# An edge-gated graph layer on one core: a new order of gates and products, of the first loads and of the table rows, and shorter edge lists

## The chip, the cores and the metric

The kernel runs on one core of one Trainium2 chip. The metric is the device time in microseconds, lower is better. An engine's instructions run in the order in which the program lists them; between engines semaphores hold an instruction until what it reads is there. The engines are TensorE (PE, with its weight loads as PEld), VectorE (DVE), ScalarE (ACT), GpSimd (POOL) and SyncE (SP), and 16 DMA engines move the data.

## The reference

One layer of a graph network over a fixed adjacency matrix. x holds 16 batches of 1024 nodes with 256 features, adj is 1024 × 1024 with about nine entries in a row, and the sum over neighbours is gated per edge and per batch:

```python
pre_u = einsum('bud,dk->buk', h, W1[:d]);  pre_v = einsum('bvd,dk->bvk', h, W1[d:])
hidden = relu(pre_u[:, :, None, :] + pre_v[:, None, :, :] + b1)
S = sigmoid(einsum('buvk,ko->buvo', hidden, W2)[..., 0] + b2[0])
a_t = einsum('buv,bud->bvd', S * A, h)
m_t = einsum('uv,bud->bvd', A, h) * h
z = beta1 * h + beta2 * (a_t @ Wa + ba) + beta3 * (m_t @ Wm + bm)
```

The kernel computes S only where A has an entry.

## The kernel before

**Tiles.** Work is cut into 32 blocks. A block is one group of four batches and one tile of 128 target nodes; each block has 10 steps, numbered n = 0 to 319 over the whole kernel (`T` = 10, `total` = 320). Groups 0 and 1 come first (six tiles each, then the last two of each), then groups 2 and 3. A step treats 128 edge slots, one edge per partition, for four batches.

**A step.** `fetch(n)` (L518, GpSimd) gathers 128 rows of 8 KB, one per edge slot, from a table in device memory that holds pre_u and h side by side. Eight buffers (`NF`) hold fetched rows, so that eight fetches are ahead. `fetch_val` (L385, GpSimd) gathers the adjacency values. `expand(n + 2)` (L607, PE) spreads pre_v of the target nodes over the edge slots into one of two PSUM buffers pc. `add(n + 1)` (L639, DVE) sums the two, `gate(n)` (four of L647, DVE) does relu and the dot product with W2, one batch each; ACT then does the sigmoid gt (L650), four scalings left (L652), and `left_adj(n + 1)` (L617), which prepares the next step's adjacency. `aggregate` (L664, PE) multiplies left with the fetched h into the accumulators, which L672 copies to ev at the end of each half.

**Products.** `products(n)` issues PE's other work of a step: pieces of table rows (`rows`: w_u products at L445, copied by ACT at L461 to one of two single tab buffers, written to the table by SP at L465), the halves of pre_v of the next block (`halves`: L445, L449, ACT copies L482, L483, L489), and the end of the block before. `turn_over` transposes ev (L682), ACT copies it to LT (L685), and one or two steps later DVE multiplies part of it by h (L696). `block_end` does the products with w_a and w_m (L713), ACT copies the result (L718), a step later DVE adds it to h_blk (L719), and SP writes it out. All these PE results go through two PSUM buffers "misc".

**Lists.** For each of the eight tiles `lists(vt)` finds the edges and their slots: L252 to L375, mostly small DVE operations, with a few matmuls and one ACT copy. Lists 0 to 3 (`EARLY`) run ahead of the first step, by the `script`; lists 4 to 7 run in pieces between gates (`fill`), begun at the steps in `start_list`. A list's first act is to load its key (L244), for lists 4 to 7 from GpSimd.

**Order.** Each engine's order is the program's, written by hand. `after(step, f)` makes f due at a step; `do(n)` issues what is due on the queue that f names (L719 and L696 on DVE; the table writes and the outputs on SP). For the main loop (L857 to L925) the order of a step is: gather in, expand(n + 2), fill, a `do(n)` ahead of the others at step 8, products(n), add(n + 1), gate(n) with the ACT work, left_adj(n + 1), do(n). In the last block only (n ≥ total − T), expand and products come after the gate. `plan` says at which step a block's hT is loaded and at which two steps its table rows are made; for the rows of group 1, L775. Ahead of the loop the script issues the eight first fetches in a row ("f"), and SP then has two hT loads and, at n = 1, w_a and w_m (L888, L889).

Of the kernel before, what the change touches and what calls it, by code (L numbers as in the profile page):

```python
# [13 lines left out]
P = 128  # L14
# [3 lines left out]
def kernel(  # L18
# [58 lines left out]
    RC = 5 + S  # L77
# [42 lines left out]
    late = fixed([P, 1], "late")  # L120
    nc.vector.tensor_scalar(late, row, float(W), None, ALU.is_ge)
    soon = fixed([P, 1], "soon")
    nc.vector.tensor_scalar(soon, row, float(W), None, ALU.is_lt)
# [77 lines left out]
    rest = const.tile([P, NT], FP, name="rest")  # L201
    nc.gpsimd.memset(val, 0.0)
# [38 lines left out]

    def lists(vt):
# [3 lines left out]
        R = lst.tile([P, RC], FP, name="R", bufs=4)  # L246
        top = R[:, 5:5 + S]
        count = lst.tile([P, 1], FP, name="count", bufs=4)
# [6 lines left out]
        nc.scalar.activation(unread, key, AF.Sign, accum_out=count)  # L255
# [24 lines left out]
        yield "op"  # L280
        nc.vector.tensor_scalar(R[:, 2:3], row, float(N), float(vt * P * N), ALU.mult, ALU.add)
        yield "op"
        nc.vector.memset(R[:, 3:4], 1.0)
        yield "op"
        nc.vector.tensor_copy(R[:, 4:5], inw)
# [17 lines left out]
        held = lst.tile([P, 1], FP, name="held", bufs=4)  # L303
# [7 lines left out]
        yield "op"  # L311
        nc.vector.tensor_tensor(rest[:, vt:vt + 1], count, held, ALU.subtract)
# [4 lines left out]
        none = lst.tile([P, 1], FP, name="none", bufs=4)  # L317
        nc.vector.tensor_scalar(none, held, 0.0, float(N + 1), ALU.is_equal, ALU.mult)
        yield "op"
        nc.vector.tensor_scalar(held, held, -1.0, None, ALU.add)  # L320
        yield "op"
        nc.vector.scalar_tensor_tensor(mark, slot, first, mark, ALU.is_ge, ALU.mult)
        yield "op"
        last = lst.tile([P, 1], FP, name="last", bufs=4)
        nc.vector.scalar_tensor_tensor(used, nth, held, top, ALU.is_equal, ALU.mult, accum_out=last)
        yield "op"
        nc.vector.tensor_tensor(thr[:, vt:vt + 1], last, none, ALU.add)
# [4 lines left out]
        for w, mine in enumerate((soon, late)):  # L332
            nc.vector.tensor_scalar(RR[:, w, :], R, mine, None, ALU.mult)
# [21 lines left out]
        nc.vector.tensor_tensor(eq, eq, L[:, :, 5:], ALU.mult)  # L355
# [7 lines left out]
        nc.vector.tensor_tensor(k_of, L[:, :, 2], k_of, ALU.subtract)  # L363
        yield "op"
        nc.vector.scalar_tensor_tensor(k_of, L[:, :, 3], -BIG, k_of, ALU.mult, ALU.add)
        yield "op"
        nc.vector.tensor_scalar(vidx[:, sl].rearrange("p w j -> p (w j)"), k_of, BIG + N, None, ALU.add)
# [4 lines left out]
        for i in range(2):  # L372
            nc.vector.tensor_tensor(
                onehot[:, sl].rearrange("p w (q i) v -> p w q i v", i=2)[:, :, :, i, :],
                place.unsqueeze(1).to_broadcast([P, NW, Q, V]),  # L375
                col[:, :, i:i + Q, 4:5].to_broadcast([P, NW, Q, V]), ALU.is_equal)
            if i == 0:
                yield "op"
# [49 lines left out]
    def load_hT(k):  # L428
        g, nt = k
        if k in aside_:  # L430
            hTs[k] = hta.tile([P, GB, DC, P], FP, name="hT_")
        else:
            hTs[k] = hT_of[k] = hT_free.pop(0)
        nc.sync.dma_start(hTs[k].rearrange("p b c n -> p (b c) n"),
                          xT_rows[:, g * GB * DC:(g + 1) * GB * DC, nt * P:(nt + 1) * P])
# [105 lines left out]
    for i in range(COPIES):  # L541
# [3 lines left out]
              "h 2 1 1", "h 2 2 3 u", "2 f 2 2 w h h h", "m 3 w 3 3 3")  # L545
# [14 lines left out]
    for t, turns_ in enumerate(script):  # L560
        step = t - 100
        do(step)
        for c in turns_.split():
# [8 lines left out]
            elif c == "h":  # L572
                go(parts, step)
            elif c == "v":
                fetch_val(T)
                spread(b1_p, b1_b)
                next(parts)
            elif c == "f":
                for n in range(NF):
                    fetch(n)  # L580
            elif c == "u":
                fetch_val(3)
            elif c == "m":
                load_mark(0)
            elif c == "w":
                warm(6)
            else:
                next(made[int(c)], None)
# [177 lines left out]
    start_list = dict(zip((0, 16, 48, 88), range(EARLY, NT)))  # L766
# [8 lines left out]
    plan(turn[NT:], ((0, 1, 8), (1, 9, 12), (9, 18, 19), (13, 22, 28), (20, 29, 32), (29, 38, 39), (33, 42, 48), (40, 49, 51)))  # L775
# [8 lines left out]
    def made_rows(n):  # L784
        nonlocal piece, last
        if n in loads:
            if loads[n] in begun and loads[n][0] == 1:
                aside_.remove(loads[n])
            load_hT(loads[n])
            if loads[n] not in begun:  # L790
                copy_h(loads[n])
                begun.add(loads[n])
# [7 lines left out]
    def products(n, k, s):  # L800
# [10 lines left out]
        if ROOM <= n < total - T:  # L811
            if s in (8, 9):
# [28 lines left out]
    ROOM, MORE, LISTS = 10, 3, 110  # L841
    ahead = NF
# [17 lines left out]
    for n in range(total + 2):  # L860
# [10 lines left out]
        if n < total - T:  # L871
            expand(n + 2)
            if n >= ROOM:
                fill(n, False)
                if s == 8:
                    do(n)
# [8 lines left out]
        if n >= total - T and n + 2 < total:  # L885
            expand(n + 2)
        if n == 1:
            w_a = load_weights(Wa, "w_a", nc.sync)  # L888
            w_m = load_weights(Wm, "w_m", nc.sync)  # L889
# [23 lines left out]
        if n < ROOM:  # L913
            fill(n, False)
        if n >= total - T:
# [6 lines left out]
        if n == 120:  # L922
            nc.gpsimd.partition_all_reduce(longest, rest, P, bass_isa.ReduceOp.max)
# [116 lines left out]
```

## Time and profile before

| | us |
|---|---|
| timed, median of 3 | 1110.08 |
| timed, lowest and highest | 1110.04, 1113.46 |
| profiled execution, its own time | 1097.05 |
| span of that execution | 1095.2 |

The mean granted TensorE clock in that execution was 0.979. The profile is of one execution. In its rows the first number is the start in us, the second the duration in us, and what stands in brackets is how long the engine sat idle before the instruction and what released it. A wait row names the waiting instruction, then what it waited for, with the total in us, the count and the longest. Start and length of the blocks, from the first add of each in the timeline:

| block | start | length | DVE idle in it |
|---|---|---|---|
| 0 | 63.48 | 39.07 | 10.74 |
| 1 | 102.56 | 35.65 | 0.14 |
| 2 | 138.20 | 37.99 | 2.17 |
| 3 | 176.19 | 35.85 | 2.49 |
| 4 | 212.04 | 30.68 | 0.97 |
| 5 | 242.72 | 37.60 | 4.44 |
| 6 | 280.32 | 33.55 | 0.00 |
| 7 | 313.87 | 30.55 | 1.09 |
| 8 | 344.42 | 30.26 | 1.30 |
| 9 | 374.68 | 32.81 | 0.00 |
| 10 | 407.49 | 37.31 | 3.05 |
| 11 | 444.80 | 30.58 | 1.27 |
| 12 to 22, mean of each | | 30.15 | 1.23 |
| 23 to 30, mean of each | | 29.92 | 0.99 |
| 31, to the end | 1046.47 | 48.78 | 9.44 |

### The profile page before, as it was taken

The page shows a single profiled execution, that of the slowest core. Times are in us where ns is not written, and L with a number is a line of the kernel's source. Part 1 is how long each engine was busy: PE and PEld are TensorE (multiplying, and loading weights), DVE is VectorE, ACT ScalarE, POOL GpSimd, SP SyncE. Part 2 cuts the span into 40 slices and gives each one's busy share as a digit, 9 for nine tenths or more (in the row PEclk, how much of TensorE's full clock was granted, in tenths as well). Part 3 has the DMA queues.
Part 4 walks back from the last instruction along what each step waited for, and adds up shares of the span by engine and source line. Part 5 has one row for each costly group of instructions (what it writes and reads, how often), then busy time and mean ns, then how long its engine had stood idle before and what let it go on. Part 6 is the DMA issues. An engine that isn't in the chain of part 4 may idle for free.

```text
span 1095.2 us, 24089 instructions
## 1 busy us (share of the span) xinstructions
PE 1029.3 (94%) x7645; PEld 735.7 (67%) x7645; DVE 1020.8 (93%) x3487; ACT 862.0 (79%) x2616; POOL 465.5 (42%) x453
## 2 busy tenths in 40 slices
PE   7876998998999999999999999999999999999986
PEld 7744766776667767677777777777766666666653
DVE  8878999998999999999999999999999999999994
ACT  3435777786889877888988888888888888888873
POOL 2746676472456324554334333333343332333320
PEclk9887999999999989999999999999999999999999
DMA  9998999999999999999999999999999999999991
GB/s 289 330 399 282 331 361 355 398 377 378 388 356 396 399 391 348 380 392 402 406 401 405 395 409 391 392 395 401 358 384 341 353 340 334 337 347 353 347 328 43
DMA packets 149032, 394.56 MB, mean 360 GB/s; under 512 B 18224, under 2 KB 96048, under 8 KB 112688
## 3 DMA queue, kind: packets, MB, share of 16 engines
q0 software_dynamic: 50240, 300.11, 69.8%
q1 hardware_dynamic: 85360, 79.71, 22.7%
q10 hardware_dynamic: 13296, 13.11, 3.7%
q8 instruction: 63, 1.03, 0.4%
q14 instruction: 73, 0.60, 0.1%
HBM read 396.93 MB, written 50.33 MB: 408 GB/s over the span
## 4 chain that ended last, share of the span: by engine, by line
PE 58%; DVE 17%; ACT 12%; DMA 8%; issue 4%; POOL 0%; DVEq 0%; SPq 0%; ACTq 0%; POOLq 0%
PE misc L713 16%; PE acc L664 14%; PE misc L445 13%; PE pc L607 9%; DVE fetched L647 7%; DVE fetched L639 6%; ACT left L652 3%; PE misc L682 2%; DMA fetched<-table,uidx 2%; PE misc L449 2%; DMA hT<-in_xT_dram 2%; ACT X L489 1%; ACT LT L718 1%; DMA table<-tab 1%; DMA key<-in_adjT_dram 1%
## 5 line engine op out<-in xcount | busy, mean ns | idle before, releaser
L518 POOL DMA_INDIRECT fetched<-table,uidx x320 | 344.9, 1078 | 534.8 <-PE acc L664 361.8
L647 DVE SCALAR_TENSOR_TENSOR fetched<-fetched,w_b 128x256 f32<-128x256 f32 x1280 | 477.1, 419 | 0.0
L639 DVE TENSOR_TENSOR fetched<-fetched,pc 128x1024 f32<-128x1024 f32 x320 | 387.9, 1212 | 11.5 <-PE pc L607 5.0
L652 ACT ACTIVATE left<-left,gt 128x32 f32<-128x32 f32 (+1 forms) x1280 | 299.5, 305 | 10.4
L664 PE MATMUL acc<-fetched,left 128*32 128x256 f32 x4096 | 287.3, 389 | 19.4 <-ACT left L652 19.3
L607 PE MATMUL pc<-X,mark 128*128 128x512 f32 x640 | 244.8, 464 | 16.2 <-DVE fetched L639 14.6
L664 PEld LDWEIGHTS acc<-fetched,left 128*32 128x32 f32 x4096 | 133.9, 110 | 131.9 <-ACT left L652 42.3
L607 PEld LDWEIGHTS pc<-X,mark 128*128 128x128 f32 x640 | 106.0, 191 | 96.4 <-issue 35.4
L650 ACT ACTIVATE gt<-sc,b_b 128x4 f32<-128x4 f32 x320 | 95.9, 300 | 57.9 <-DVE fetched L647 55.1
L713 PE MATMUL misc<-w_m,LT 128*128 128x256 f32 x496 | 117.3, 379 | 0.0
L713 PE MATMUL misc<-w_a,LT 128*128 128x256 f32 x496 | 117.2, 379 | 0.0
L445 PE MATMUL misc<-w_v,hT 128*128 128x256 f32 x448 | 107.6, 384 | 0.0
L713 PEld LDWEIGHTS misc<-w_a,LT 128*128 128x128 f32 x496 | 94.0, 190 | 15.1 <-ACT LT L685 0.4
L713 PEld LDWEIGHTS misc<-w_m,LT 128*128 128x128 f32 x496 | 94.1, 190 | 14.8
L385 POOL DMA_INDIRECT val<-in_adjT_dram,vidx x80 | 89.8, 1122 | 33.6 <-issue 16.1
L617 ACT ACTIVATE left<-onehot,val 128x64 f32<-128x64 bf16 (+1 forms) x320 | 102.9, 322 | 0.0
L647 DVE DVE_READ_ACCUMULATOR fetched<-fetched,w_b 128x1 f32 x1280 | 101.7, 79 | 0.0
L445 PEld LDWEIGHTS misc<-w_v,hT 128*128 128x128 f32 x448 | 86.3, 193 | 13.8
L682 PE MATMUL misc<-ident,ev 128*128 128x128 f32 x512 | 79.8, 279 | 10.8 <-ACT tab L461 5.5
L682 PEld LDWEIGHTS misc<-ident,ev 128*128 128x128 f32 x512 | 61.5, 142 | 37.8 <-ACT ev L672 15.4
L482 ACT CAST X<-misc 128x512 fp32r<-128x512 f32 x64 | 37.3, 583 | 59.8 <-PE misc L445 59.7
L685 ACT COPY LT<-misc 128x512 f32<-128x512 f32 x128 | 73.1, 572 | 7.0 <-PE misc L682 5.9
(178 smaller groups left out, 1006.1 us busy)
## 6 DMA issues: line engine op xcount, KB each, us to landing
h_blk<-table SPq DMA_DIRECT2D x62, 256.0 KB, 9.8
out_dram<-h_blk SPq DMA_DIRECT2D x62, 256.0 KB, 12.6
hT<-in_xT_dram SPq DMA_DIRECT2D x28, 512.0 KB, 20.5
table<-in_x_dram ACTq DMA_DIRECT2D x24, 512.0 KB, 13.8
table<-tab SPq DMA_DIRECT2D x48, 256.0 KB, 11.1
fetched<-table,uidx POOLq DMA_INDIRECT x320
table<-in_x_dram SPq DMA_DIRECT2D x8, 512.0 KB, 11.6
table<-fetched SPq DMA_DIRECT2D x8, 512.0 KB
```

The costliest lines, as they stand in the source:

```text
L385: nc.gpsimd.indirect_dma_start(out=val[:, i, j:j + 1], out_offset=None, in_=adj_flat, in_offset=bass.IndirectOffsetOnAxis(ap=vidx[:, i, j: ...
L445: nc.tensor.matmul(p[:, bb * D:(bb + 1) * D], hT[:, 2 * h + bb, i, :], wt[:, i, :], start=(i == 0 and not begun), stop=(i == DC - 1), skip ...
L518: nc.gpsimd.indirect_dma_start(out=fetched[at_slot[n]], out_offset=None, in_=table[g], in_offset=bass.IndirectOffsetOnAxis(ap=uidx[:, vt * ...
L607: nc.tensor.matmul(pcs[n][:, c], marks[n // TW][:, j * P:(j + 1) * P], cuts[k][:, w, c], start=True, stop=True)
L617: nc.scalar.activation(lefts[n][:, :m, 1::GB, :], onehot[:, i, o:o + m, :].unsqueeze(2).to_broadcast([P, m, GB // 2, V]), AF.Copy, scale=v ...
L639: nc.vector.tensor_tensor(t, t, pcs.pop(n), ALU.add)
L647: nc.vector.scalar_tensor_tensor(t[:, b, :], t[:, b, :], 0.0, w2_b, ALU.max, ALU.mult, accum_out=sc[:, b:b + 1])
L650: nc.scalar.activation(gt, sc, AF.Sigmoid, bias=b2_b)
L652: nc.scalar.activation(lefts[n][:, :m, 2 * b, :], lefts[n][:, :m, 1 + b // 2 * GB, :], AF.Copy, scale=gt[:, b:b + 1])
L664: nc.tensor.matmul(accs[h][b * 2 * V:(b + 1) * 2 * V, r, :], left[:, i, 2 * b - b % 2:2 * b - b % 2 + 2].rearrange("p k v -> p (k v)"), f[ ...
L682: nc.tensor.transpose(pt[:, r, :, c, :], ev[:, r, c * P:(c + 1) * P], ident)
L713: nc.tensor.matmul(pz[:, bb * D:(bb + 1) * D], LTs[k][:, 2 * h + bb, i if bb else 1 - i, c, :], wt[:, c, :], start=False, stop=(i == 0 and ...
```

## The change

Four things are changed.

1. *Order.* `LAST` = 230 takes the place of total − T: from block 23 on, fill, expand(n + 2) and products(n) are issued after add(n + 1), gate(n) and do(n). In blocks 1 to 22 the first `turn_over` of a block (step 8) is issued after gate(8) and do(8), and the extra do at step 8 is gone, so that what is due there (the second L719 of the block) comes behind add(9) and gate(8).
2. *First loads.* hT of the tenth turn, w_a and w_m are loaded on GpSimd between fetch 2 and fetch 3; list 4's key is loaded there between fetch 5 and fetch 6. hT of the ninth turn stays on SP ("k" in the script).
3. *Steps.* New steps for the table rows of group 1, and lists 4 to 7 begin at 7, 18, 48, 86 in place of 0, 16, 48, 88.
4. *Shorter lists.* What is the same for all lists is made once; one `tensor_tensor` makes both halves of RR; one operation makes vidx in place of three; thr and rest are finished for all lists at n = 120 with three operations.

On PE the sequence of one step's kinds of work stays as it was except where pieces of lists and rows move with their steps; what moves in part 1 are ACT's copies against gt, left and left_adj, and DVE's h_blk adds.

```diff
-    RC = 5 + S
+    RC = 4 + S
...
+    Rs = [lst.tile([P, RC], FP, name=f"R{i}") for i in range(EARLY)]
...
-        nc.vector.tensor_scalar(R[:, 2:3], row, float(N), float(vt * P * N), ALU.mult, ALU.add)
-        yield "op"
-        nc.vector.memset(R[:, 3:4], 1.0)
-        yield "op"
-        nc.vector.tensor_copy(R[:, 4:5], inw)
+        if vt < EARLY:
+            nc.vector.tensor_scalar(R[:, 2:3], row, float(N), -BIG, ALU.mult, ALU.add)
+            nc.vector.tensor_copy(R[:, 3:4], inw)
...
-        nc.vector.tensor_tensor(rest[:, vt:vt + 1], count, held, ALU.subtract)
...
-        nc.vector.tensor_scalar(none, held, 0.0, float(N + 1), ALU.is_equal, ALU.mult)
-        nc.vector.tensor_scalar(held, held, -1.0, None, ALU.add)
...
-        nc.vector.scalar_tensor_tensor(used, nth, held, top, ALU.is_equal, ALU.mult, accum_out=last)
-        nc.vector.tensor_tensor(thr[:, vt:vt + 1], last, none, ALU.add)
+        nc.vector.scalar_tensor_tensor(used, upto[:, 1:S + 1], held, top, ALU.is_equal, ALU.mult, accum_out=thr[:, this])
...
-        for w, mine in enumerate((soon, late)):
-            nc.vector.tensor_scalar(RR[:, w, :], R, mine, None, ALU.mult)
+        nc.vector.tensor_tensor(RR, R.unsqueeze(1).to_broadcast([P, NW, RC]),
+                                half_of.unsqueeze(2).to_broadcast([P, NW, RC]), ALU.mult)
...
-        nc.vector.tensor_tensor(k_of, L[:, :, 2], k_of, ALU.subtract)
-        nc.vector.scalar_tensor_tensor(k_of, L[:, :, 3], -BIG, k_of, ALU.mult, ALU.add)
-        nc.vector.tensor_scalar(vidx[:, sl].rearrange("p w j -> p (w j)"), k_of, BIG + N, None, ALU.add)
+        nc.vector.scalar_tensor_tensor(vidx[:, sl].rearrange("p w j -> p (w j)"), L[:, :, 2],
+                                       BIG + N + float(vt * P * N), k_of, ALU.add, ALU.subtract)
...
                 for n in range(NF):
                     fetch(n)
+                    if n == 2:
+                        load_hT(turn[NT + 1], nc.gpsimd)
+                        w_a = load_weights(Wa, "w_a", nc.gpsimd)
+                        w_m = load_weights(Wm, "w_m", nc.gpsimd)
+                    elif n == 5:
+                        next(made[EARLY])
+            elif c == "k":
+                load_hT(turn[NT])
...
-    start_list = dict(zip((0, 16, 48, 88), range(EARLY, NT)))
+    start_list = dict(zip((7, 18, 48, 86), range(EARLY, NT)))
...
-    plan(turn[NT:], ((0, 1, 8), (1, 9, 12), (9, 18, 19), (13, 22, 28), (20, 29, 32), (29, 38, 39), (33, 42, 48), (40, 49, 51)))
+    plan(turn[NT:], ((1, 2, 4), (2, 8, 9), (5, 12, 18), (10, 19, 22), (20, 28, 29), (23, 32, 38), (30, 39, 42), (40, 48, 49)))
...
         if ROOM <= n < total - T:
-            if s in (8, 9):
+            if s == 9 or s == 8 and n >= LAST:
                 turn_over(k, 0, s - 8, n)
...
+    LAST = (BS - NT - 1) * T
...
-        if n < total - T:
+        if n < LAST:
             expand(n + 2)
             if n >= ROOM:
                 fill(n, False)
-                if s == 8:
-                    do(n)
             products(n, k, s)
...
         do(n)
-        if n >= total - T and n + 2 < total:
+        if s == 8 and ROOM <= n < LAST:
+            turn_over(k, 0, 0, n)
+        if n >= LAST and n + 2 < total:
             expand(n + 2)
         if n == 1:
-            w_a = load_weights(Wa, "w_a", nc.sync)
-            w_m = load_weights(Wm, "w_m", nc.sync)
...
-        if n < ROOM:
+        if n < ROOM or n >= LAST:
             fill(n, False)
-        if n >= total - T:
+        if n >= LAST:
             products(n, k, s)
...
         if n == 120:
+            nc.vector.tensor_tensor(rest, rest, kept, ALU.subtract)
+            nc.vector.tensor_scalar(kept, kept, 0.0, float(N + 1), ALU.is_equal, ALU.mult)
+            nc.vector.tensor_tensor(thr, thr, kept, ALU.add)
```

## The prediction

> **What bounds the kernel now.** I read the page's first part, then cut the span by blocks. A block is 10 steps, and it starts with its first add (L639) in the timeline.
>
> ```profile
> span 1095.2 us, 24089 instructions
> PE 1029.3 (94%) x7645; PEld 735.7 (67%) x7645; DVE 1020.8 (93%) x3487; ACT 862.0 (79%) x2616; POOL 465.5 (42%) x453
> ```
>
> PE and DVE are equally full over the span, so the average names no bound. The windows of five blocks (0, 5, 6, 16, 24) do; the columns are the window, its length, busy time of PE, PEld, DVE, ACT, POOL, granted clock, DMA share and GB/s.
>
> ```profile
> 63.48:102.56 39.08, 29.13 (x151) 18.53 (x152) 30.98 (x108) 21.17 (x64) 19.73 (x23) 0.73 0.91 342
> 242.72:280.32 37.60, 33.81 (x253) 24.43 (x244) 33.16 (x120) 27.83 (x84) 13.29 (x13) 0.95 1.00 365
> 280.32:313.87 33.55, 31.90 (x243) 22.40 (x240) 33.55 (x122) 26.41 (x81) 13.70 (x17) 1.00 1.03 397
> 596.04:626.19 30.15, 30.08 (x237) 21.93 (x232) 28.89 (x98) 26.34 (x82) 11.23 (x10) 1.00 1.02 398
> 837.05:866.96 29.91, 28.60 (x219) 19.61 (x216) 28.91 (x98) 25.64 (x79) 10.23 (x10) 1.00 0.96 369
> ```
>
> Block 6 has DVE without a gap: lists bound it. Blocks 0 and 5 are neither full of DVE nor of PE: something stalls. Block 16 leaves DVE 1.26 us, but PE is full. Block 24 has 1.3 us of PE free and 1.00 of DVE idle: there DVE's wait sets the time. Which waits these are, the waits of DVE say (total, times, longest):
>
> ```profile
> DVE h_blk L719 <- ACT LT L718: 29.6, 25, 2.5
> DVE LT L696 <- ACT LT L685: 7.4, 4, 2.9
> DVE key L252 <- DMA key<-in_adjT_dram: 6.3, 2, 5.8
> DVE fetched L639 <- PE pc L607: 5.0, 3, 3.0
> DVE fetched L639 <- DMA fetched<-table,uidx: 3.9, 2, 2.2
> DVE fetched L639 <- issue: 2.6, 1, 2.6
> ```
>
> The timeline gives their places:
>
> ```profile
> 73.43 0.56 POOL L244 DMA_DIRECT2D key<-in_adjT_dram  x1 [2.05 <-DMA fetched<-table,uidx]
> 86.15 0.69 DVE L252 SCALAR_TENSOR_TENSOR key<-key,ukey 128x512 f32<-128x512 f32 x1 [5.79 <-DMA key<-in_adjT_dram]
> ...
> 256.33 0.58 ACT L461 COPY tab<-misc 128x512 f32<-128x512 f32 x1 [5.18 <-DMA table<-tab]
> 256.97 0.66 PE L682 MATMUL misc<-ident,ev 128*128 128x128 f32 x4 [3.50 <-ACT tab L461]
> ...
> 863.16 0.59 ACT L718 COPY LT<-misc 128x512 f32<-128x512 f32 x1 [0.16 <-PE misc L713]
> 863.78 0.75 DVE L719 SCALAR_TENSOR_TENSOR h_blk<-h_blk,be,LT 128x512 f32<-128x512 f32 x1 [1.00 <-ACT LT L718]
> ```
>
> Three kinds are to be seen: DVE waits for list 4's key, which GpSimd issues only after all eight first fetches; a table-row copy waits for its single buffer and takes PE and DVE with it; and once a block, the second h_blk add waits for a copy made just before it.
>
> **The sum, part by part.** It is made against the profiled execution (1097.05 us, span 1095.2) and carried over to the median of 1110.08; the 13 us between them I can't attribute, so I assume that they stay.
>
> *Loads and list 4.* Stalls of block 0: 1.70 at 66.41 (fetch 1), 0.36, 5.79 (key); ahead of it the first add waits 2.65. Sum 10.5. The 1 MB of w_a, w_m and hT that SP issues at 45.7–53.4 goes on GpSimd's queue between fetches 2 and 3. A direct load there took 0.56 us (key row); three take 1.7 us if the many-piece hT load costs the same. It has eight times the pieces of a whose load, unseen here, so from 0.56 to about 4.5 us (8 × 0.56); I take the low end, nearest to the key row. Queued behind them on GpSimd are fetches 3 to 7, list loads and vals; adds 3 to 7 wait for those fetches. The Trainium skill ("DMA: Bandwidth & Descriptors", Issuing engines are not separate DMA queues) speaks against a gain: another issuer still uses the same 16 DMA engines. The row: fetch 3, issued at 57.72, landed at 70.59, 12.87 us later, so the engines are indeed the limit. By the rule alone the bytes are only reordered and the gain at the first adds is 0; by the order, fetches 0 to 2 pass 1 MB, and what they gain comes back at adds 3, 6 and 7. I weigh it so: the initial stalls go, about 2.5 us return (1 MB at block 0's 342 GB/s is 3 us). The key is different: it is issued about 10 us earlier and is needed later (list 4 now starts at step 7), so 5.79 goes. Against it, some 1.2 us of list 4's DVE work slides into block 1. Sum: −10.5 + 2.5 + 1.2 ≈ −7.0; ends −3 (GpSimd slow, so that fetches 24–25 come late after it has run back to back) and −10.
>
> *Shorter lists.* Lists 4 to 7, which run between gates, lose 10 small DVE operations each. Duration and cost differ:
>
> ```profile
> 402.80 0.15 DVE L281 TENSOR_SCALAR R<-rows 128x1 f32<-128x1 f32 x1
> 402.86 0.42 DVE L647 SCALAR_TENSOR_TENSOR fetched<-fetched,w_b 128x256 f32<-128x256 f32 x1
> ```
>
> L281 lasts 0.15, but the next gate starts 0.06 after it. The skill ("VectorE: DVE Perf Modes", The TRN2 errata) gives 58 cycles plus the elements at 0.96 GHz, an estimate of 61 ns for 128x1: it agrees with the start to start, not with the duration. By durations (about 0.15 each) four lists would save 6 us; by start to start (0.06–0.07 mostly, 0.10 for the 128x10 ones, 0.15 for L333, nothing for the memset) it is 0.73 a list, 2.9 in all. I take −2.9. That is in list blocks, which DVE bounds, so it counts whole; were PE the cover there, 0. The early lists, ahead of the first add, wait for loads: 0 (at most −0.5). Three added 128x8 operations at step 120 cost 0.2 inside a PE-bound block: 0.
>
> *Second h_blk behind gate(8), table rows at other steps* (blocks 1 to 10). Waits of L719 on L718 in blocks 3, 4, 5: 2.49 + 0.97 + 1.08 = 4.54. Behind gate(8) the copy has a whole step (3 us) of head start: they go. The tab stall in block 5 arises as the second piece for one tab buffer came 3 steps after the first, while its write took 13.63 us to land; the new plan keeps 4 or more between pieces of the same half, and where it is 4 today (steps 8 and 12, 28 and 32) no copy waits: 2.84 goes (1.26 + 1.58, both behind the copy at 256.33). Blocks 7, 8 are near PE's limit: 0.4 each of 1.1–1.3. Sum −8.2; ends −4 (the new plan brings a wait for tab or hT elsewhere) and −9. Block 2's 2.17 (a fetch late) I leave: 0. Block 10's 3.05 stands in a half-clock stretch with the scores behind L461 and L685; L685 now goes behind gate 8 and the pieces are over earlier: −1.0, ends 0 and −3.
>
> *Blocks 11 to 22.* The same move removes 1.25 per block from DVE. But PE's own start-to-start work there is about 29.7 of 30.15; what is left beside it is 0.45, of which 0.17 is a wait that this move removes (L664 waits for lefts queued behind L685, which now come ahead of it). 12 × 0.17 = −2.0; ends 0 and 12 × 0.45 = −5.4. L685 behind gate(8) is late for L696 by at most a gate; that is two steps later.
>
> *Gates first, blocks 23 to 30.* Here no table rows are left, PE needs about 26.4 by starts, ACT 25.6, DVE 28.9. ACT now does gt (0.30), four lefts (0.96) and L617 (0.30) ahead of L718 (0.59): the copy is done about 2.1 after gate(7); DVE reaches the h_blk add about 2.5 after gate(7), behind add(9) and gate(8) (1.2 + 4 × 0.34): margin 0.4. So 0.99 goes, and the lefts come no later: 8 × 0.99 = −7.9; ends −4 and −8. Queued behind on ACT are the copies that free PE's two misc banks; PE has 2.5 us a block to wait for them. DMA moves 369 GB/s in these blocks and has moved 398. Block 31 was already in this order: 0.
>
> Sum: −7.0 − 2.9 − 8.2 − 1.0 − 2.0 − 7.9 = **−29.0**. Profiled execution about 1068; median 1110.08 − 29.0 = **1081**, own range 1075–1088.
>
> **Rivals.** *Supply gives it back* (18%): GpSimd runs back to back over 126–157 us and DMA share is 0.91–1.03; if the first fetches only change places, the 7.0 falls away and 1 of the plan's gain: 1089. For it the rule above; against it the key stall, which is order alone. *Gates first gains nothing* (13%): ACT's copies, late, hold misc banks as long as h_blk waited: −21.1, 1089. For it ACT at 86% of the block; against it PE's 2.5 us of slack. *Middle blocks gain fully* (10%): PE's busy rows are modelled ends, so its floor may be lower; −5.4 in place of −2.0, block 10 with −3 and block 0 with −10: 1081 − 3.4 − 2 − 3 = about 1073. *Slower* (5%): in blocks 23 to 30 each product's copy waits behind gt, left and L617, 1.6 us; where PE's next product, and behind it pc for the add, waits for that bank in two steps of ten, a block is 3.2 longer: 8 × 3.2 − 21.1 = +4.5, 1114.6. It decides from 3.05 us a block, (21.1 + 3.3)/8. *No difference* (4%): what holds the timed runs 13 us above the profile is not in these views and sets the time in both.
>
> **How the numbers follow.** Forecast 50%, the others as above. The three runs spread by 0.3%, 3.3 us, about what can be told from no change. Faster: 50 + 18 + 13 + 10 = 91%, same 4%, slower 5%. The range runs from the middle case with the other parts at their good ends (1070) to the two losses of 1089 together with a bad plan (1099); outside it remain about 15%.
>
> **What would show it.** Block 0 about 31–33 us without a 5.8 us key wait; no L461 wait on table<-tab near block 5; no L719 wait on L718 after block 2; middle blocks about 30.0; late blocks about 28.9 with DVE full. The prediction is wrong if fetch waits on L639 grow in blocks 0 to 2, if late blocks stay at 29.9 with L639 waiting for pc, or if PE waits on misc copies.

## The result, and the profile after

The changed kernel took 1098.74 us (median of six runs, 1095.86 to 1103.5), the kernel before 1110.6 in the same comparison: ratio 0.9895, interval 0.9867 to 0.9923. That is 11.9 us faster in the medians, where 29 were forecast. The direction was right; the size was less than half.

The profile's first part and the windows of blocks 0, 1, 5, 6, 16 and 24 of the changed kernel (columns as before: window, length, busy PE, PEld, DVE, ACT, POOL, clock, DMA share, GB/s):

```profile
span 1094.1 us, 24009 instructions
PE 1027.1 (94%) x7645; PEld 730.8 (67%) x7645; DVE 1015.7 (93%) x3418; ACT 863.1 (79%) x2616; POOL 460.7 (42%) x456
```

```profile
63.41:100.71 37.30, 31.26 (x184) 19.55 (x184) 29.36 (x94) 20.62 (x63) 22.22 (x23) 0.91 1.02 394
100.71:144.72 44.01, 39.64 (x246) 27.75 (x247) 37.21 (x132) 29.12 (x87) 26.22 (x25) 0.88 0.82 282
249.94:282.86 32.92, 32.38 (x263) 22.44 (x257) 32.85 (x116) 28.45 (x89) 11.89 (x11) 1.00 1.03 407
282.86:315.89 33.03, 31.01 (x237) 21.48 (x234) 33.03 (x117) 26.60 (x82) 14.99 (x17) 1.00 1.03 383
601.51:631.65 30.14, 30.07 (x234) 21.87 (x233) 28.94 (x96) 26.33 (x82) 10.83 (x10) 1.00 1.03 411
843.41:872.28 28.87, 27.66 (x218) 18.98 (x217) 28.87 (x97) 25.73 (x79) 10.21 (x10) 1.00 0.97 371
```

The late block is what was forecast: 28.87, DVE without a gap. Block 5 lost its table-row stall. But block 1, which had no stall before, is 44.01 long with 6.8 us of DVE idle inside it, at 0.88 of the clock. The waits of DVE (total, times, longest):

```profile
DVE fetched L634 <- PE pc L602: 30.3, 29, 2.4
...
DVE LT L691 <- ACT LT L680: 6.6, 4, 2.9
DVE fetched L634 <- issue: 4.9, 2, 3.8
DVE fetched L634 <- PE acc L659: 4.4, 2, 2.7
```

The h_blk waits (29.6 us) and the key wait (6.3) are gone from the list, and in their place the add waits 30.3 us for pc. Some 13 of that lie in blocks 12 to 22, where PE is the limit and the wait only shows it; 16.7 lie in blocks 0 to 11, where the kernel before waited 5.0 for it.

One thing has to be known to read the sums. The profiled execution of the kernel before took 1097.05 us, 13 less than any of the six timed beside the changed kernel, and 7.8 less than the fastest (1104.81) of 26 on another chip. The stalls that the forecast counted were those of that one execution.

### The profile page after: what moved, and what is told of

Its sections match the earlier page's. It is cut to its first block, busy times and chain, and to the rows that moved or that the text cites. A ratio compares the mean times of both kernels' runs of the same rounds, so it can differ in the third digit from the quotient of the medians.

```text
span 1094.1 us, 24009 instructions
## 1 busy us (share of the span) xinstructions
PE 1027.1 (94%) x7645; PEld 730.8 (67%) x7645; DVE 1015.7 (93%) x3418; ACT 863.1 (79%) x2616; POOL 460.7 (42%) x456
## 3 DMA queue, kind: packets, MB, share of 16 engines
q8 instruction: 63, 1.03, 0.4%
## 4 chain that ended last, share of the span: by engine, by line
PE 51%; DVE 31%; ACT 9%; issue 7%; DMA 1%; another core or an unknown queue 0%; ACTq 0%; DVEq 0%
PE misc L432 14%; DVE fetched L642 14%; PE acc L659 12%; DVE fetched L634 11%; PE misc L708 11%; PE pc L602 8%; ACT left L647 2%; PE misc L677 2%; PE misc L436 2%; ACT X L476 1%; DVE low L471 1%; DVE LT L691 1%; DVE h_blk L714 1%; ACT ev L667 1%; ACT gt L645 1%
## 5 line engine op out<-in xcount | busy, mean ns | idle before, releaser
L634 DVE TENSOR_TENSOR fetched<-fetched,pc 128x1024 f32<-128x1024 f32 x320 | 387.9, 1213 | 46.4 <-PE pc L602 30.3
L659 PE MATMUL acc<-fetched,left 128*32 128x256 f32 x4096 | 279.5, 387 | 10.0 <-issue 4.0
L602 PE MATMUL pc<-X,mark 128*128 128x512 f32 x640 | 244.8, 464 | 14.6 <-DVE fetched L634 12.7
L659 PEld LDWEIGHTS acc<-fetched,left 128*32 128x32 f32 x4096 | 128.4, 110 | 120.7 <-issue 33.6
L372 POOL DMA_INDIRECT val<-in_adjT_dram,vidx x80 | 86.5, 1081 | 31.7 <-issue 21.0
```

The source lines that it names most:

```text
L372: nc.gpsimd.indirect_dma_start(out=val[:, i, j:j + 1], out_offset=None, in_=adj_flat, in_offset=bass.IndirectOffsetOnAxis(ap=vidx[:, i, j: ...
L602: nc.tensor.matmul(pcs[n][:, c], marks[n // TW][:, j * P:(j + 1) * P], cuts[k][:, w, c], start=True, stop=True)
L634: nc.vector.tensor_tensor(t, t, pcs.pop(n), ALU.add)
L659: nc.tensor.matmul(accs[h][b * 2 * V:(b + 1) * 2 * V, r, :], left[:, i, 2 * b - b % 2:2 * b - b % 2 + 2].rearrange("p k v -> p (k v)"), f[ ...
```

## The experiments

Every ratio is to runs of the kernel before on the same chip. The groups of runs had different chips, so what is compared from one group to another is the ratio, and a difference in us is then the difference of the ratios times 1110. A range behind a ratio is its 95% interval. The first four take the change apart.

**Gates first from block 23 alone.**

```diff
+    LAST = (BS - NT - 1) * T
...
-        if n < total - T:
+        if n < LAST:
...
-        if n >= total - T:
+        if n >= LAST:
```

> The kernel before with gates first from block 23 alone; blocks 1 to 22 keep their order, lists, loads and steps are the old ones. Theory A (the late blocks gave what the profile after shows, 29.92 to 28.87 us each, and nothing else lasting): 7 x 1.05 and a little at block 23, 7.5 to 8.5 us faster, so about 1102.5, and nearly the whole of the measured 11.9. Theory B (the late order helps only together with the other parts): within 3 us of before.

Measured: 1101.61, ratio 0.9932 (0.9905 to 0.9959): 7.5 us, as both the forecast (7.9) and theory A had it. Up to block 22 this program is the kernel before, so its profile is a second look at that kernel. Its windows of blocks 2, 15 and 24:

```profile
139.25:183.22 43.97, 37.76 (x272) 26.78 (x274) 35.59 (x130) 28.70 (x86) 28.37 (x29) 0.88 0.83 283
577.27:608.16 30.89, 30.70 (x237) 22.00 (x232) 28.95 (x96) 26.44 (x82) 10.37 (x10) 1.00 1.01 393
849.62:878.49 28.87, 27.68 (x218) 19.00 (x217) 28.87 (x97) 25.73 (x79) 10.22 (x10) 1.00 0.97 370
```

Block 2 is 43.97 long here and was 37.99; block 23 starts at 820.74 and started at 807.12. The 13.6 us between them match the 13 us between the first profile and the timed runs: they lie in blocks 1 to 22, in waits that come at other places in each execution. What the largest one looks like, in the timeline of block 2:

```profile
159.12 1.00 POOL L385 DMA_INDIRECT val<-in_adjT_dram,vidx  x1 [0.30 <-issue]
...
159.63 1.22 DVE L639 TENSOR_TENSOR fetched<-fetched,pc 128x1024 f32<-128x1024 f32 x1 [2.99 <-PE acc L664]
...
161.02 0.41 PE L664 MATMUL acc<-fetched,left 128*32 128x256 f32 x2 [0.80 <-issue]
...
162.44 0.59 PE L664 MATMUL acc<-fetched,left 128*32 128x256 f32 x1 [1.01 <-issue]
163.09 1.00 POOL L385 DMA_INDIRECT val<-in_adjT_dram,vidx  x1 [0.31 <-issue]
165.30 0.59 ACT L482 CAST X<-misc 128x512 fp32r<-128x512 f32 x1 [9.54 <-remote]
165.35 1.22 DVE L639 TENSOR_TENSOR fetched<-fetched,pc 128x1024 f32<-128x1024 f32 x1 [2.35 <-remote]
```

PE starts an instruction or two at a time and waits for nothing that the profile shows; ACT and DVE start again within 0.05 us of each other, ACT after 9.54 us.

**The second h_blk add behind gate(8), in blocks 1 to 30.**

```diff
-            if s in (8, 9):
+            if s == 9 or s == 8 and n >= LAST:
...
+    LAST = total - T
...
             if n >= ROOM:
                 fill(n, False)
-                if s == 8:
-                    do(n)
...
+        if s == 8 and ROOM <= n < LAST:
+            turn_over(k, 0, 0, n)
...
```

> The kernel before with the second h_blk add and the first turn-over of a block behind gate(8) in blocks 1 to 30, all else old. By the forecast's terms (4.54 + 0.8 in blocks 3 to 8, 2.0 in 11 to 22, 1.0 in block 10, and 0.99 each in 23 to 30 since the add has a step more there too) 16 faster, 1094. Theory A (a wait on PE or on a fetch takes the place of the h_blk wait in the blocks up to 22, the late blocks gain): 6 to 9 faster. If it gains under 3, PE or ACT was the limit everywhere.

Measured: 1092.81, ratio 0.9864 (0.9834 to 0.9894), 15.1 us (16.7 in the medians). The forecast's terms stand in their sum. This move alone is faster than the whole change by the medians (the intervals overlap), and it gains most of what gates first gains too: its late blocks are 29.05 us in the mean of 23 to 30, against 28.87 with gates first.

**The shorter lists alone** (all of the change's edits in `lists`, with the three operations at step 120).

> The kernel before with the shorter lists alone. By the forecast 2.9 faster, 1107.5. Theory A (in list blocks a DVE burst that ends earlier only waits for PE or a fetch): 0 to 1.5 faster. By the durations of the profile's rows it would be 6.

Measured: 1115.43, ratio 1.0058 (1.0035 to 1.008): 6.4 us slower. None of the expectations had this sign.

**Loads and steps** (first loads on GpSimd, new list starts, new steps for the table rows).

> The kernel before with the first loads on GpSimd, the new list starts and the new steps for the table rows, order and lists old. By the forecast 7.0 + 2.84 faster, 1100.5. Theory A (what block 0 saves comes back in blocks 1 to 11 as fetches that are late and as PE held at half clock after gaps): within 3 us of before. Slower than before by over 3 would say that the new steps cost by themselves.

Measured: 1102.42, ratio 0.9936 (0.9915 to 0.9958): 7.1 faster. Theory A, that nothing is kept, falls; 7.1 of 9.8 is kept.

So the lists are where the forecast fails most. A list's pieces are issued one to a gap between gates; with fewer operations it runs through its gaps sooner, and its matmuls, its ACT copy, its GpSimd casts and loads and its gathers of values all come earlier: in the profile, list 5's second matmuls come about five steps earlier (step 32 against 37). The next run separates content from pace.

```diff
         nc.vector.tensor_scalar(used, top, 0.0, None, ALU.is_gt, ALU.add, accum_out=R[:, 0:1])
+        for _ in range(3):
+            yield "op"
...
         nc.vector.tensor_scalar(mark, slot, R[:, 0:1], None, ALU.is_lt)
-        yield "op"
+        for _ in range(3):
+            yield "op"
...
```

> The shorter lists alone, but with an empty slot left where an operation is gone, so that PE, ACT, GpSimd and SyncE have the same order as before at the same steps; only DVE has less to do. Theory P (the shorter lists alone were 6 slower because their pieces on PE, ACT, GpSimd and the DMA queues come up to five steps earlier and meet the table rows): 2 to 4 faster than before, as the forecast had it, about 1106.5. Theory O (an operation of the new lists, or the tiles that they now share, costs more than it saves): 4 to 7 slower, as the shorter lists alone were. Between -1 and +1: the saved DVE time is given back as a wait for PE.

Measured: 1111.11, ratio 0.9993 (0.9974 to 1.0012). So content costs nothing and gains nothing (within about 2 us); the pace costs the 6. It is the third case of the expectation: the saved DVE time is given back.

**The changed kernel with the old lists.**

> The changed kernel with the old lists: order, loads and steps are new. By the forecast's term it would be 2.9 slower than the changed kernel, 1101.6. If the parts' single effects add (the shorter lists alone +5.9), 1093, faster than both kernels. If the other parts do not add among themselves, 1098 to 1100.

Measured: 1092.8, ratio 0.9831 (0.9798 to 0.9864): 7.1 faster than the change as a whole.

**The order alone** (both order edits; lists, loads and steps old).

> Only the order: gates first from block 23 and the second h_blk add behind gate(8) in blocks 1 to 22; lists, loads and steps old. The forecast's terms give 8.2 - 2.84 + 1.0 + 2.0 + 7.9 = 16.3 faster than before, 1093.3; by the single runs the same, since the h_blk move alone (to block 30) gave 16.7. If this is as fast as the kernel with loads and steps too, those add nothing once the order is new.

Measured: 1095.32, ratio 0.9852 (0.981 to 0.9895): 16.4 us. The forecast's terms for these edits sum to 16.3; the interval is about 5 us wide on each side.

**The first loads alone** (hT, w_a, w_m and list 4's key on GpSimd; list 4 begins at step 0 as before).

```diff
                 for n in range(NF):
                     fetch(n)
+                    if n == 2:
+                        load_hT(turn[NT + 1], nc.gpsimd)
+                        w_a = load_weights(Wa, "w_a", nc.gpsimd)
+                        w_m = load_weights(Wm, "w_m", nc.gpsimd)
+                    elif n == 5:
+                        next(made[EARLY])
...
```

> Only the first loads on GpSimd and list 4's key between fetches 5 and 6; list starts and steps of the table rows old, so list 4 still begins at once. The forecast's 7.0 for block 0 belongs to this part (its key stall and its fetch stalls): 1102.5 if it stands alone. If the gain of loads and steps together (7.1) was that of the steps, within 2 of before here.

Measured: 1117.16, ratio 1.0044 (1.002 to 1.0068): 4.9 slower. The timeline of block 0:

```profile
68.37 0.59 POOL L244 DMA_DIRECT2D key<-in_adjT_dram  x1 [0.65 <-DMA fetched<-table,uidx]
...
82.29 0.69 DVE L252 SCALAR_TENSOR_TENSOR key<-key,ukey 128x512 f32<-128x512 f32 x1 [11.15 <-DMA key<-in_adjT_dram]
```

The key is asked for 5 us earlier than before (68.37 against 73.43) and lands 13.9 us after that, where it took 12.7 before; DVE waits 11.15 for it instead of 5.79. But this edit moves more than the loads. With the load already issued, what list 4 does first at step 0 is L252 itself: it stands behind 2 adds here, behind 6 before, behind 9 in the changed kernel, where it waits for nothing. The 5.4 us of added waiting are about as much as the run lost, so the loss can be the price of reading the key too early; what the moved loads cost by themselves this run does not show.

**Order with the new steps, loads on SyncE**, and **the steps alone.**

> The new order with the new list starts and table-row steps; the first loads stay on SyncE and list 4's key is loaded when the list begins, at step 7; lists old. Theory K (moving the loads gives nothing, as the bytes go through the same DMA engines: alone it was 4.9 slower; what loads and steps gave together came from list 4 beginning later): 1088 to 1092, no slower than order with loads and steps (1092.8). Theory S (loads and steps need each other, since list 4's key, asked for at step 7, then comes late): 1095 to 1100.

> The kernel before with the new list starts and table-row steps alone. Theory K: 7 to 12 faster than before (7.1 with the loads, which alone cost 4.9). Theory S: within 3 of before.

Measured: 1084.64, ratio 0.9771 (0.9733 to 0.9808), and 1099.87, ratio 0.9897 (0.9865 to 0.9929). Theory K's direction holds in both (the first is 3 us below the range it gave): the steps give 11.4 alone and more without the moved loads than with them, by 4.3 in the old order (11.4 against 7.1) and 6.7 in the new one (0.9771 against 0.9831), though in each pair the intervals overlap a little. The place is the start: block 2 begins at 135.5 to 137.7 us in the four profiles of all runs that have the new steps and the loads on SyncE, and at 138.5 to 145.8 in the eight that have the new steps and the moved loads. In the four, list 4's key is also read four steps later (behind 13 adds), so the loads and that delay are not separated. Order with steps is as fast as any whole kernel here: by the ratio 25 us faster than before, 14 faster than the change.

**The changed kernel with the lists at the old pace.**

> The changed kernel whole, but with an empty slot left in the lists where an operation is gone. Theory P (the pace of the shorter lists is what costs, not their content): as with the old lists, 1091 to 1095. If the new lists' content costs in this kernel: 1097 to 1100, as the changed kernel.

Measured: 1086.47, ratio 0.9782 (0.975 to 0.9815), 4.5 us under theory P's range. In the whole kernel the quick pace costs 12.5 us (0.9895 against 0.9782), twice what it costs alone. Against the old lists it is 5.4 faster (0.9831; the intervals overlap), so that here the shorter content may gain what the forecast gave it; a run below, with the loads on SyncE, does not repeat this. The profiled execution, the slowest of this run's five (1094.08), shows the next thing that is late, in block 14:

```profile
545.56 3.78 PE L439 MATMUL misc<-w_v,hT 128*128 128x256 f32 x8 [9.82 <-DMA hT<-in_xT_dram]
549.38 0.59 ACT L476 CAST X<-misc 128x512 fp32r<-128x512 f32 x1 [12.05 <-PE misc L439]
550.08 1.22 DVE L641 TENSOR_TENSOR fetched<-fetched,pc 128x1024 f32<-128x1024 f32 x1 [10.16 <-PE pc L609]
```

Here PE waits for an hT load in a stretch where the DMA engines are full (540 to 542: share 1.03, 412 GB/s) and no engine works.

**The lists made longer** (the kernel before, nine more small operations in each of lists 4 to 7, on scratch columns, in the slots of those that the change takes away).

```diff
+    def more(n, times):
+        idle = ones[:, :n] if n == 1 else from_q[:, :n]
+        for _ in range(times):
+            nc.vector.tensor_scalar(idle, upto[:, :n], 1.0, None, ALU.mult)
...
         nc.vector.tensor_scalar(R[:, 2:3], row, float(N), float(vt * P * N), ALU.mult, ALU.add)
+        if vt >= EARLY:
+            more(1, 1)
```

> The kernel before with nine more small DVE operations in each of lists 4 to 7 (on scratch columns, issued in the slots of those that the change takes away), all else the same: about 0.7 us of DVE a list, 2.8 in all, the forecast's own price with the sign turned. If DVE bounds the list blocks in most executions, as the forecast's term for the lists took it: 2.8 slower. If the time goes to waits on PE and on DMA queues, which other executions show in blocks 2 to 5: within 1.5 of before, as shortening them at the old pace changed nothing.

Measured: 1109.24, ratio 1.0005 (0.999 to 1.002): +0.5, not +2.8. A DVE microsecond in the list blocks is not a microsecond of the kernel: added, it did not cost, and taken away at the old pace, in the kernel before, it did not gain.

**Which lists, and the loads in the whole kernel.** Four runs: the old pace in lists 4 and 5 alone, in 6 and 7 alone, the changed kernel with the loads back on SyncE, and that with the old pace in all lists.

> The changed kernel with the old pace (empty slots) in lists 4 and 5 alone, which run in blocks 0 to 4; lists 6 and 7 keep the quick pace. If the pace costs through meetings in the crowded first blocks (fetches, vals, table writes and loads at once): near 1086.5, as with all lists at the old pace. If it costs in blocks 5 to 11: near 1098.7, as the changed kernel.

> The changed kernel with the old pace in lists 6 and 7 alone (blocks 4 to 11). The mirror of the run before: near 1098.7 if the first blocks are the place, near 1086.5 if it is blocks 5 to 11, about 1092 in both runs if the cost is spread.

> The changed kernel with the first loads on SyncE again and list 4's key asked for when the list begins; order, steps and the shorter lists at their quick pace stay. By the single runs (loads alone +4.9; order and steps with old lists 1084.6 against 1092.8 with the loads): about 1090, 8 faster than the changed kernel. If the loads matter only with the old lists: 1097 to 1100.

> Order, steps and the shorter lists at the old pace, the first loads on SyncE: the parts that helped, without the two that did not. If the effects add: 1084.6 (order and steps with old lists) less 0 to 3 for the shorter lists, 1082 to 1085, the forecast's own range. If the pace and the loads are one and the same cost (both make GpSimd's queue and the first blocks' transfers meet), no better than 1086.5.

Measured: 1100.16 (0.9889, 0.9863 to 0.9915); 1092.9 (0.9844, 0.9812 to 0.9876); 1090.38 (0.9812, 0.9774 to 0.985); 1087.09 (0.978, 0.9752 to 0.9809). The old pace in lists 4 and 5 alone gains nothing; in lists 6 and 7 it gains half, so blocks 5 to 11 hold at least that half, and the effects don't add. The loads cost 9 in the changed kernel and nothing once the pace is old (0.978 against 0.9782), and the quick pace costs 12.5 with the moved loads and 3.6 without them (0.9812 against 0.978, intervals that overlap): the two costs are not separate. Shorter lists at the old pace give nothing beside the order and the steps (0.978 against 0.9771). Block 7 shows the pace best. Its windows in the changed kernel, in the run with lists 4 and 5 at the old pace, and in the run with lists 6 and 7 at it:

```profile
315.89:348.89 33.00, 29.62 (x198) 21.16 (x195) 29.35 (x97) 24.19 (x73) 19.76 (x18) 0.95 0.94 334
```

```profile
319.98:356.08 36.10, 29.99 (x198) 21.11 (x195) 29.41 (x96) 24.05 (x73) 19.56 (x18) 0.91 0.86 318
```

```profile
314.98:344.30 29.32, 28.25 (x193) 20.13 (x192) 29.32 (x98) 24.02 (x73) 20.15 (x18) 1.00 0.98 359
```

The work is the same (DVE 29.3 to 29.4); where list 6 runs quickly, 3.7 and 6.7 us of waiting are added. This holds over all profiles that have the gathers of adjacency values: in block 7 DVE is idle for 2.3 to 6.7 us in the four where list 6 runs quickly, for 0.0 to 1.4 in the fourteen where it doesn't. In each of these three windows GpSimd has 18 operations: ten fetches and eight gathers of adjacency values (L385 before).

**Without the gathers.** In the profiles of all these kernels up to here 67 adds waited over 1.4 us between blocks 1 and 22. For 52 of them a gather of values was issued in the 4 us before the wait began, or during it. Of the time of blocks 1 to 22 only about 26% lies within 6 us behind such a gather. That comparison is weaker than it looks: nearly all gathers, and 66 of the 67 waits, lie in blocks 1 to 11, and there it is 48% of the time.

```diff
-        for i, j in wanted[:n]:
-            nc.gpsimd.indirect_dma_start(
-                out=val[:, i, j:j + 1], out_offset=None, in_=adj_flat,
...
         del wanted[:n]
```

> The changed kernel without the 80 gathers of adjacency values (all left out, the values stay zero, so the output lacks the sums over neighbours); all else the same. In the profiles so far 52 of 67 waits of an add over 1.4 us between blocks 1 and 22 have such a gather issued in the 4 us before or within them, though only about 26% of that time lies within 6 us behind one. Theory V (the gathers' transfers of single elements hold up what is late in these places, and the quick pace and the moved loads cost by where the gathers fall): 1075 to 1082, the long waits in blocks 1 to 11 mostly gone. Theory D (any late transfer under the load of the fetches does it): 1090 or more, no more than the GpSimd time that goes.

> The changed kernel with the lists at the old pace, and without the gathers of adjacency values as in the run before. Theory V: within 3 us of the run before, since the 12 us between quick and old pace came through the gathers. If it is 8 to 14 faster than the run before, the pace costs by other means (PE's and ACT's pieces).

Measured: 1080.76 and 1087.02, on a chip where the kernel before took 1100.13 (ratios 0.9818, 0.9785 to 0.9852, and 0.9888, 0.9848 to 0.9928). Neither expectation is met as it stands. 1080.76 lies in theory V's range only because this chip is faster; by the ratio the gain is 20.2, 8.5 more than the changed kernel's, 1090 on the scale of the others, where theory D begins. The second run is 6 us slower than the first, neither within 3 of it nor 8 to 14 faster. Block 7 of the first of the two:

```profile
305.64:334.46 28.82, 28.82 (x204) 21.15 (x200) 28.82 (x96) 24.78 (x77) 11.27 (x10) 1.00 1.03 390
```

The waiting of block 7 is gone with the eight gathers. Block 11, 34.69 with 5.34 us of DVE idle in the changed kernel, is 28.87 with none, and 28.82 with the old pace. Over blocks 1 to 11 DVE is idle for 9.8 us, 6.6 of them in block 1, against 25.4 in the changed kernel; at the old pace it is 16.3 without the gathers and 16.2 with them. Block 1, the longest of the changed kernel, is as long without the gathers, 43.76 and 43.48. It need not be for the same reason. Its window in the first run, and ACT's copies of table rows in the first and the second:

```profile
96.11:139.87 43.76, 33.95 (x229) 24.26 (x231) 37.16 (x135) 26.85 (x82) 8.94 (x10) 0.88 0.85 312
```

```profile
108.19 0.59 ACT L443 COPY tab<-misc 128x512 f32<-128x512 f32 x1 [10.00 <-DMA table<-tab]
```

```profile
110.04 0.58 ACT L450 COPY tab<-misc 128x512 f32<-128x512 f32 x1 [11.83 <-DMA table<-tab]
```

This is the stall of the single tab buffer. The pieces are at steps 4 and 9 of the new plan, and the write of the first took 27.5 us to land (80.65 to 108.11) and 27.8 in the second run.

So for block 7 it is shown, as far as profiles of several chips can show it, that the waiting needs both the quick pace and the gathers (their transfers or the 86.5 us of GpSimd time that go with them, which no run separates). For the 12.5 us of the whole kernel it is not shown. With the gathers the quick pace costs, without them it is 6 us faster than the old one; but the two pairs ran on different chips, no kernel with the gathers but the one before ran on this one, and by the ratios the old pace does worse without the gathers (0.9888) than with them (0.9782), which nothing here explains. In both runs blocks 14 and 15, where no gather runs in any kernel, lose 9 to 11 us of DVE time, in the first of them in part to a late hT load that PE waits 3.6 us for.

## Why the prediction was wrong, step by step

The shares of the measured gain, one part added to the next by the ratios (each times 1110): order 16.4 (0.9852), loads and steps with it 2.3 more (0.9831), shorter lists 7.1 lost (0.9895). Sum 11.6, the measured gain. Against the forecast of 29.0 the order is right (16.3), the lists miss by 10.0 (2.9 gained was forecast), and loads and steps by 7.5 (9.8 was forecast).

**Order: right in the sum.** Forecast 16.3, measured 16.4, with 5 us of uncertainty. Gates first: 29.92 to 28.87 in blocks 24 to 30, as reckoned from the order gt, lefts, L617, L718 against add, gate. The margin of 0.4 us is seen after: ACT's copy for h_blk (L713 there) comes behind gt and the lefts, and the add (L714) starts without a wait:

```profile
864.32 0.56 ACT L713 COPY LT<-misc 128x512 f32<-128x512 f32 x1
...
865.92 0.74 DVE L714 SCALAR_TENSOR_TENSOR h_blk<-h_blk,be,LT 128x512 f32<-128x512 f32 x1
```

The second h_blk add: its waits are gone in every block. In blocks 11 to 22 PE remains the limit, as said, but the gain is larger than 2.0. Blocks 12 to 22 are 30.43 to 30.65 us in the mean in seven other profiles of kernels with the old order; the profile that I read had 30.15, the fewest waits of all. With the new order nine profiles have 30.03 to 30.26 (three more have a long stall in blocks 14 and 15). That is some 0.4 us a block, near the end of 5.4 that the forecast gave this term: in size the rival *Middle blocks gain fully* came true here, though not by its reason: the blocks did not end lower than reckoned, they began higher than the one profile showed. As the sum still fits, other terms of the order may have given less; which, no run tells.

**Shorter lists: the step that failed most.** "I take −2.9. That is in list blocks, which DVE bounds, so it counts whole" was wrong twice. Nine operations more did not cost it and ten fewer did not gain it: block 6, which I showed as the evidence for DVE, is without a gap in every execution, and there the lists at the old pace did gain 0.4 us (33.18 against 33.56 in the second execution of the old order); but the other list blocks, 1 to 5 and 7 to 11, have waits on PE and on transfers of 2 to 10 us in one execution or another, and what DVE saves goes into those. And the step left out what the list's generator moves: the small operations were also the slots that paced the list's work for other engines. The missing slots bring the gathers and the rest up to five steps forward, and that cost 6.4 us alone and 12.5 in the whole. By which of the moved pieces is shown in block 7 alone (the gathers); elsewhere it stays open. The text costed every DVE instruction that was removed and none of those that moved with it. The price of a small operation, 60 to 70 ns from start to start, did not matter, since the microsecond saved was not DVE's to give.

**Loads and list 4: the stalls went, the time did not.** Of 9.8 for loads and steps 7.1 came alone, 2.3 behind the new order. The waits that the term of 7.0 named are gone in the changed kernel: the first add, the add of fetch 1 and the key wait for nothing, and 1.4 us come back at adds 3 and 5. But the first add starts where it did (63.41, before 63.48), adds 9 and 10 then wait 3.77 and 2.67, and block 1 has 6.80 us of DVE idle where it had 0.14. So block 2 begins at 144.72, not some 7 us ahead of the 138.20 of before. The step that failed is to put the stalls of the first adds down as time gained: waits of the same size came later in blocks 0 and 1. Why they come there is open but for the two runs without the gathers, where a table row waits for its buffer. The rule that I weighed, that another issuing engine gives no other DMA engines (the Trainium skill, "DMA: Bandwidth & Descriptors", Issuing engines are not separate DMA queues), agrees with the key: asked for 5 us earlier, it took 13.9 us to land where it had taken 12.7. "It is issued about 10 us earlier and is needed later" put two causes together. Issued early and read at step 0, it gained nothing; the later start of list 4 with the new steps for the table rows gave 11.4 with all loads on their old engines, and these two are not separated.

**Ends of blocks 3 to 10.** The stall of the single tab buffer was seen in block 5 of the profile before and in block 5 of the shorter lists alone (10.65 us, behind a SyncE that took 7.3 us to issue an output), but not in the second execution of the old order. With the new steps it did not come back in block 5, but in the two runs without the gathers it came at step 9, as shown above: "the new plan brings a wait for tab or hT elsewhere", the end that the forecast put at −4. (In the changed kernel another stall ends just before that copy, so it can't be seen there.) The plan left 4 steps or more between pieces, by a write that took 13.63 us to land; there a write took 27.5.

**The base.** All of this was reckoned on one execution that lacked 13 us of waits which the timed runs have; I noted the 13 us and assumed that they stay. They are waits in blocks 1 to 22, so some of the parts meet them: the order gained there, the pace lost there. *No difference* named these 13 us as what could set the time in both; of the other rivals *Supply gives it back* (1089) was nearest in mechanism, with the first loads only changing places, but it looked at the fetches, for which the adds hardly wait in the changed kernel, and it gave the lists their 2.9.

Three kernels that leave out either the quick pace or the moved loads come to 1084.6, 1086.5 and 1087.1, ratios 0.977 to 0.978. Where the forecast had 29 in mind, the parts that help give 24 to 25.

## What to carry to other kernels

An operation in a schedule that hands out pieces by slots is also a delay for everything behind it: when a piece is removed, keep the slot empty first, measure, and only then let the rest move up. Before a sum is made on stalls of one profile, look at a second execution; a stall that sits elsewhere there is not the place's, and removing its nearest cause gains little. A load that is issued earlier can push back what stood behind it, and in a hand-written schedule its first user may move with it: look at both before the wait that went is put down as a gain.

## What was not expected of the hardware

In stretches of 3 to 6 us PE starts an instruction or two each 0.7 to 1.4 us without a wait that the profile shows, and ACT, DVE and GpSimd resume within a microsecond of each other (165.30 and 165.35 in the timeline above; likewise at 100.7 to 100.9 in block 1 of the changed kernel):

```profile
100.80 0.59 ACT L448 COPY tab<-misc 128x512 f32<-128x512 f32 x1 [7.86 <-PE acc L659]
```

Half the clock follows (0.51 granted from 100.71 to 103.00), 10.2 us of it in block 1 of the changed kernel. Many of these stretches stand near the gathers of 128 single values, but block 1 has as much half clock without the gathers (10.2 us, behind the wait for a tab buffer), so the cause of these stretches stays open.

The kernel before itself took 1108.9 to 1111.9 us in the medians on the chips of five of the comparisons and 1100.1 on the chip of the last two runs. Blocks 23 to 30, which have hardly a wait, take 28.96 us each in the two profiles from there, as in the others with both order edits (28.96 to 28.97), so what differs is the waits and not the pace of the work. On which chip the first profile was taken is not known; on that one its 1097.05 would be usual. Ratios on one chip are what compares, and where waits are the subject even these only in part.
